# Moving the next layer's keys and values behind the expert slots, and the ternary weights into an earlier region, in a four-layer gated cross-attention kernel

## The chip, the cores and the metric

The kernel runs on one core of a Trainium2 chip. The metric is the device time of one execution in microseconds (us). Before the change it is 1820.37 us, the median of three runs (1815.41 to 1821.47).

## What is computed

The input `x` holds 8 sequences of 256 positions with 256 features; a context of the same shape supplies keys and values. Four layers follow one another. Each adds a gated cross-attention (16 heads of 16 features) and then a gated feed-forward part:

```python
x = x + jnp.tanh(g_xattn[0]) * _L0_xattn_ref(_layernorm(x, axis=-1), ctx_1024, ctx_1024, mask_Bx1xSxS2_ik1)
x = x + jnp.tanh(g_ffn[0]) * _L0_ffn_ref(_layernorm(x, axis=-1), ...)
x = x + jnp.tanh(g_xattn[1]) * _L1_xattn_ref(_layernorm(x, axis=-1), ctx_1024, ctx_1024, ...)
x = x + jnp.tanh(g_ffn[1]) * _L1_ffn_ref(_layernorm(x, axis=-1), L1_ffn_Wr, L1_ffn_W1, L1_ffn_b1, L1_ffn_W2, L1_ffn_b2)
x = x + jnp.tanh(g_xattn[2]) * _L2_xattn_ref(_layernorm(x, axis=-1), ctx_1024, ...)
x = x + jnp.tanh(g_ffn[2]) * _L2_ffn_ref(_layernorm(x, axis=-1), ...)
x = x + jnp.tanh(g_xattn[3]) * _L3_xattn_ref(_layernorm(x, axis=-1), ctx_1024, ...)
x = x + jnp.tanh(g_ffn[3]) * _L3_ffn_ref(_layernorm(x, axis=-1), L3_ffn_w1, L3_ffn_conv_w, L3_ffn_conv_b, L3_ffn_w2)
```

The feed-forward parts of layers 1 and 2 choose two of eight experts for each of the 2048 tokens. That of layer 1 has 1024 hidden units an expert:

```python
logits = x_flat @ Wr
w, ind = jax.lax.top_k(logits, K)
w = jax.nn.softmax(w, axis=-1)
combine = jnp.einsum('tke,tk->te', jax.nn.one_hot(ind, E, dtype=x.dtype), w)

def body(acc, params):
    W1e, b1e, W2e, b2e, ce = params
    h = jax.nn.gelu(x_flat @ W1e + b1e, approximate=False)
    y = h @ W2e + b2e
    return (acc + ce[:, None] * y, None)
```

That of layer 2 does the same with 512 hidden units and a norm of its own. That of layer 3 rounds its weights to -1, 0 and 1, scaled by the mean of their magnitudes, so all of a weight matrix has to be summed before it is used.

## The kernel before

**Stages.** Region 1 holds attention layers 0 and 1, feed-forward 0 and the routing of layer 1 (0 to some 620 us). The first expert layer follows (to 922 us), then region 2, attention layer 2 with the routing of layer 2 (to 1226), the second expert layer (to 1390), and region 3, attention layer 3 with the ternary feed-forward (to the end). Below, "seam 1" and "seam 2" are the two passages from an attention layer to an expert layer.

**Attention.** `attention` (L223) works through one batch element after another ("job"), 16 heads each. The clock of its plan is the unit: one unit is one head of one element. `plan(at, f)` (L600) puts a piece of work at a unit number into `todo`, and `run` issues, for each unit, the scores (`sc`), the probabilities (`st`, exponentials `pT`), the values (`po`) and then that unit's pieces. The order of PE's matmuls is pinned: `mm` and `turn` keep them in program order. The order on DVE, ACT and SP isn't pinned; a scheduler places those instructions, apart from single ones wrapped in `pin`. Indirect gathers on POOL are pinned.

**Setting up a layer.** `setup(l)` (L234) fetches the four weight matrices and the biases, and also forms the bias product: `pgb`, up to three pairs of matmuls of the broadcast value bias with `wo`, plus the output bias, scaled by DVE into `gb`. For the layer after an expert layer it can't be planned inside that layer's own region; it goes into the list `early`. So do the keys and values of that layer's first two elements, K by `proj("k", 0)` and `proj("k", 1)`, V by `vals(0)` and `vals(1)`. `early` thus has nine entries: the setup, four for element 0 and four for element 1. `tail(early, end)` (L1387) gives each of them a unit past the end of the region (offsets 11, 12 to 15, and 23 to 26).

**The K stack.** After both halves of K, `stack` (L259) splits them into three bf16 pieces (`pc_k`, lines L201 to L204, on POOL unless another engine is named), writes them to DRAM (`dr_k`, 384 KB, L281) and reads them back rearranged with six DMAs (`kstack`, L288). All of these are issued on SP. Q goes the same way (`pc_q`, `dr_q`, `qstack`); for the first element after an expert layer in two halves, on DVE.

**Routing.** `routing` (L771) treats four blocks of 512 tokens, two elements each. Its steps stand at units counted from the block's end: `norm`, `normT` (transposes `pt_f`), `out` (router logits `plf`), `choose` (a chain of small DVE steps on the logits, ending in `rtf_run`), `weigh`, `rank` (matmuls `rankf`), and `place` and `tabulate` for both halves (matmuls `tabf` into `rt_table`). The last block's steps lie past the region's end, among `early`.

**Slots and experts.** `slots` (L958) sums the tokens of each expert (matmul `tot`), derives the expert of each slot of 128 tokens (`sl_...`, `wrow`) and the token at each place (matmul `tok`, cast to `toki`), and where each token's results will be (`rt_si`). `experts` then gathers expert weights (`we`) and tokens (`xg`) by indirect DMAs on POOL, transposes the tokens (`ptg`, `xgT`), and runs `phg`, the activation `hg` and `yg`; results (`ysb`) are stored to DRAM (`yd`, by SP). At the start of the next region each element gathers its two results a token (`yg<-yd`) and adds them to `x` (L1158).

**Ternary weights.** `ffn3` (L1170) has `ternary`, which returns for each of two matrices `fetch` (1 MB by SP, `f3raw`, L1191 to L1193), `total` (the sum of magnitudes on DVE, `wab`, L1200), `mean`, and four `quarter` steps that round. They are handed to the second expert layer as `between`, each with the number of the tile at which it is issued.

Of the kernel before, what the change touches and what calls it, by code (L numbers as in the profile page):

```python
# [17 lines left out]
B, S, D = 8, 256, 256  # L18
NH, DK = 16, 16
# [12 lines left out]
AHEAD, VLAG = 3, 1  # L32
# [6 lines left out]
def kernel(ctx: ExitStack, tc: tile.TileContext, a: dict, out: bass.AP):  # L39
# [20 lines left out]
    nc = tc.nc  # L60
# [18 lines left out]
    for b in range(B):  # L79
        for i in range(2):  # L80
            t = 2 * b + i
# [52 lines left out]
    tg = const.tile([P, 8], F32, tag="tg", name="tg")  # L134
    nc.scalar.activation(tg, graw, AF.Tanh)

    def load(name, shape, src):
        t = const.tile(shape, F32, tag=name, name=name)
        nc.scalar.dma_start(t, src)
        return t  # L140

    def row(name):
        t = small.tile([1, D], F32, tag="row", name=f"row_{name}", bufs=1)
        nc.scalar.dma_start(t, a[name].rearrange("(o n) -> o n", o=1))
        return t
# [77 lines left out]
    def attention(layers):  # L223
# [7 lines left out]
        pool = None  # L231
        lay = {}

        def setup(l):  # L234
            y = lay[l] = {"bq": None, "bk": None}
            for n in "qkvo":
                w = awpool.tile([P, DC, D], F32, tag=f"w{n}", name=f"w{n}{l}")
                nc.sync.dma_start(w, a[f"L{l}_w{n}"].rearrange("(c p) o -> p c o", p=P))
                y[n] = w
            bv = None  # L240
            if l in (1, 3):
                y["bq"] = load(f"bq{l}", [P, DC], a[f"L{l}_bq"])
                nc.vector.tensor_scalar(y["bq"], y["bq"], 1.0 / DK**0.5, None, ALU.mult)
                y["bk"] = load(f"bk{l}", [P, DC], a[f"L{l}_bk"])
                bv = load(f"bv{l}", [P, DC], a[f"L{l}_bv"])


            bo = row(f"L{l}_bo")
            pb = bank(ps_m, "m", f"pgb{l}")[:, :D]
            if bv is not None:  # L250
                for c in range(DC):
                    bvb = keep.tile([P, P], F32, tag="bvb", name=f"bvb{l}_{c}", bufs=2)
                    nc.vector.tensor_copy(bvb, bv[:, c : c + 1].to_broadcast([P, P]))
                    mm(pb, bvb, y["o"][:, c, :], c == 0, False)
            mm(pb, ones[0:1, :], bo, bv is None, True)
            y["gb"] = keep.tile([P, D], F32, tag="gb", name=f"gb{l}")
            nc.vector.tensor_scalar(y["gb"], pb, tg[:, l : l + 1], None, ALU.mult)
# [36 lines left out]
        lead = layers[0] > 0  # L294

        def prep(j, l, b):
# [96 lines left out]
            def proj(s, oc):  # L393

                if oc == 0:
                    o["p"] = bank(ps_m, "m", f"p{s}_{n}").rearrange("p (c s) -> p c s", c=DC)
                    o["t"] = keep.tile([P, DC, S], F32, tag=f"{s}T", name=f"{s}T_{n}")
                src = o["xs"] if s == "q" else ctxT[b]
                for c in range(DC):
                    mm(  # L400
                        o["p"][:, oc, :], lay[l][s][:, c, oc * P : (oc + 1) * P], src[:, c, :],
                        c == 0, c == DC - 1,
                    )
                bias = lay[l][f"b{s}"]
                scale = 1.0 / DK**0.5 if s == "q" else 1.0
                dst = o["t"][:, oc, :]
                if bias is not None:
                    nc.scalar.activation(  # L408
                        dst, o["p"][:, oc, :], AF.Identity, bias=bias[:, oc : oc + 1], scale=scale
                    )  # L410
                elif s == "q":
                    nc.scalar.mul(dst, o["p"][:, oc, :], scale)
                else:
                    nc.scalar.copy(dst, o["p"][:, oc, :])
                if s == "q" and lead and j == 0:

                    o["qs"] = stack(o["t"], s, j, oc, nc.vector)
                elif oc:
                    o[f"{s}s"] = stack(
                        o["t"], s, j, engine=nc.vector if s == "q" and lead and j == 1 else None  # L420
                    )

            def vals(i):
# [168 lines left out]
        todo, early = {}, []  # L592
# [7 lines left out]
        def plan(at, f, *args):  # L600
            todo.setdefault(at, []).append(lambda: f(*args))

        for j, (l, b) in enumerate(jobs):
            if l and b == 0:
                if j:
                    plan(NH * (j - 2) - AHEAD - 6, setup, l)
                else:
                    early.append(lambda l=l: setup(l))
            for at, f in prep(j, l, b):
                plan(NH * (j - 2) - AHEAD + at, f)  # L610
            for c in range(DC):
                at = slot[NH * j + HC * c + HC - 1] + 1
                plan(at, parts, j, c)
                plan(at + (3 - (c == 0) if j == 0 else 4), rows, j, c)
            for at, f in finish(j, l, b):
                plan(NH * (j + 1) + at, f)
# [154 lines left out]
    def routing(l, pool, xd, gate, at0):  # L771
# [22 lines left out]
        def block(blk):  # L794
# [140 lines left out]
            def tabulate(h):  # L935
# [12 lines left out]
            at = at0 + NH * (2 * blk + 2)  # L948
            return [
                (at + 11, norm), (at + 19, lambda: normT(0)), (at + 20, lambda: normT(1)),  # L950
                (at + 22, out), (at + 23, choose), (at + 26, weigh), (at + 30, rank),
                (at + 32, lambda: place(0)), (at + 36, lambda: tabulate(0)),
                (at + 37, lambda: place(1)), (at + 41, lambda: tabulate(1)),
            ]

        return w, [(at0, load_weights)] + [q for blk in range(NB) for q in block(blk)]
# [213 lines left out]
    def ffn3(home):  # L1170

        nh = 8
        w = {}

        def hbuf(name):
            return home.tile([P, nh, S], F32, tag="f3h", name=name, bufs=2)
# [5 lines left out]
        def ternary(n, at):  # L1182
# [35 lines left out]
            def quarter(k):  # L1218
# [4 lines left out]
                    q[:, k * BLK : (k + 1) * BLK], t, RND, None, ALU.subtract  # L1223
                )

            return [(0, fetch), (at, total), (at + 1, mean)] + [
                (at + 2 + k, lambda k=k: quarter(k)) for k in range(4)
            ]

# [143 lines left out]
        def pieces(pool):  # L1373
            return [q for b in range(B) for q in element(pool, b)]

        return [(0, load_weights)] + ternary(1, 8) + ternary(2, 16), pieces

    def moe(l, nh, nsets, apart, w, xd, between=(), scale=None):
        with tc.tile_pool(name=f"c{l}", bufs=1) as pool:
            with tc.tile_pool(name=f"rt{l}", bufs=1) as tmp:  # L1380
                rows = slots(l, pool, tmp, w, nsets)
            with tc.tile_pool(name=f"f{l}", bufs=1) as tiles:
                return experts(l, tiles, xd, w["c"], rows, nh, scale, between, nsets, apart)

# [1 line left out]

    def tail(early, end):  # L1387

        at = [11, 12, 13, 14, 15, 23, 24, 25, 26]
        return [(end + k, f) for k, f in zip(at, early)]  # L1390

    early, run = attention((0, 1))
# [1 line left out]
    with tc.tile_pool(name="r1", bufs=2) as pool:  # L1394
        w, pieces = routing(1, pool, xd[0], tg[:, 5:6], NH * B)
        run(pool, ffn0(pool) + pieces + tail(early, 2 * NH * B))
    ahead = moe(1, 8, 3, True, w, xd[0])
    early, run3 = attention((3,))
    with tc.tile_pool(name="r2", bufs=2) as pool:
        w, pieces = routing(2, pool, xd[1], tg[:, 6:7], 0)  # L1400
        run2(pool, pieces + tail(early, NH * B), ahead)
    with tc.tile_pool(name="f3w", bufs=1) as home:
        weights, pieces = ffn3(home)
        ahead = moe(2, 4, 5, False, w, xd[1], weights, w["nw"])
        with tc.tile_pool(name="r3", bufs=2) as pool:
            run3(pool, pieces(pool), ahead)


def _layout(inputs):
# [85 lines left out]
```

## Time and profile before

| what | us |
|---|---|
| median of three runs | 1820.37 |
| the profiled execution | 1816.64 |
| its span, first to last instruction | 1814.8 |
| first expert layer, PE without a break | 647.2 to 920 |
| last yd store of the first expert layer | 922.60 |
| first nm of attention layer 2 | 949.75 |
| wo for the bias product, issue at seam 2 | 1191.18 |
| second expert layer, PE without a break | 1244.6 to 1390 |

The profiled execution is one of the kernel's runs; times of single instructions come from it. TensorE's mean granted clock over it was 0.898. The busy rows cut the span into 40 slices of 45 us, one digit each, in tenths:

```profile
DVE  4655554444767511111137767752422767778777
ACT  0354544555556133333314544512231256555641
POOL 2352232232330244343334453014553445554452
DMA  6654222222541444242224535027341444222000
GB/s 165 150 152 99 69 60 59 60 60 59 129 131 30 112 150 138 88 135 85 85 71 111 132 96 140 17 78 244 99 149 56 129 100 102 66 56 57 7 6 18
```

The slices from 14 to 20 are the first expert layer: DVE has little to do there. Slice 28 (1225 to 1270 us) holds the start of the second expert layer and the greatest DMA traffic of the kernel, 244 GB/s. A row of the timeline reads: start, length, engine, line, operation, output and inputs, shapes, count; in brackets how long the engine stood idle before it, and what ended that.

### The profile page before, as it was taken

What the parts mean: (1) busy time and instruction counts of PE and PEld (TensorE: products, weight loads), DVE (VectorE), ACT (ScalarE), POOL (GpSimd) and SP (SyncE); (2) the same over time, 40 slices, a digit from 0 to 9 for tenths busy, and PEclk for the clock granted to TensorE, in tenths of its full rate; (3) what the DMA queues carried; (4) which work ended last, traced back from release to release, by engine and by line L of the source; (5) the groups of instructions that cost most, each with busy time, mean ns of one, the idle gap of its engine ahead of it and who ended that gap; (6) DMA issues with size and microseconds to landing.
All of it is one profiled execution on the core that took longest, in us unless ns stands there. A gap on an engine that the chain in (4) does not pass through costs nothing.

```text
span 1814.8 us, 27468 instructions
## 1 busy us (share of the span) xinstructions
PE 1446.9 (80%) x9888; PEld 1097.3 (60%) x9918; DVE 946.7 (52%) x2918; ACT 742.2 (41%) x1629; POOL 679.9 (37%) x816
## 2 busy tenths in 40 slices
PE   1689888999998599999957888866997587776653
PEld 1356666676665399999944555546996454454432
DVE  4655554444767511111137767752422767778777
ACT  0354544555556133333314544512231256555641
POOL 2352232232330244343334453014553445554452
PEclk9899999999999799999978988977998788888876
DMA  6654222222541444242224535027341444222000
GB/s 165 150 152 99 69 60 59 60 60 59 129 131 30 112 150 138 88 135 85 85 71 111 132 96 140 17 78 244 99 149 56 129 100 102 66 56 57 7 6 18
DMA packets 101116, 170.11 MB, mean 94 GB/s; under 512 B 26642, under 2 KB 85141, under 8 KB 90197
## 3 DMA queue, kind: packets, MB, share of 16 engines
q1 hardware_dynamic: 71759, 113.93, 25.7%
q0 software_dynamic: 23664, 52.81, 8.9%
q10 hardware_dynamic: 5558, 1.63, 0.4%
q8 instruction: 78, 1.28, 0.3%
q14 instruction: 57, 0.47, 0.1%
HBM read 224.69 MB, written 41.68 MB: 147 GB/s over the span
## 4 chain that ended last, share of the span: by engine, by line
PE 59%; DVE 20%; DMA 8%; POOL 5%; issue 4%; ACT 3%; SPq 1%; ACTq 0%; POOLq 0%; DVEq 0%
PE phg L192 11%; PE yg L192 11%; PE po L192 5%; PE y_f L192 4%; PE st L192 4%; PE ph_f L192 4%; PE sc L192 4%; PE pv L192 3%; PE pk L192 3%; DVE nm L479 3%; PE pq L192 3%; DMA qstack<-mt 2%; DVE ms L474 2%; DMA kstack<-dr_k_None 1%; DMA xg<-xd,toki 1%
## 5 line engine op out<-in xcount | busy, mean ns | idle before, releaser
L523 ACT ACTIVATE pT<-st 128x512 f32<-128x512 f32 x512 | 298.9, 597 | 286.7 <-PE st L192 244.8
L479 DVE TENSOR_REDUCE nm<-sc 128x2 f32<-128x512 f32 x384 | 256.9, 681 | 119.7 <-PE sc L192 118.7
L192 PE MATMUL sc<-kstack,qstack 112*128 112x256 bf16 x1024 | 213.1, 297 | 95.5 <-DMA kstack<-dr_k_None 28.1
L1105 ACT ACTIVATE hg<-phg,we 128x128 f32<-128x128 f32 x468 | 133.5, 368 | 283.9 <-issue 259.6
L192 PE MATMUL st<-qstack,kstack 115*128 115x256 bf16 x1024 | 210.2, 290 | 44.3 <-ACT pT L523 23.6
L192 PEld LDWEIGHTS phg<-xgT,we 128*128 128x128 f32 x1872 | 224.3, 195 | 7.2 <-DVE xgT L1087 1.8
L192 PE MATMUL phg<-xgT,we 128*128 128x128 f32 x1872 | 225.8, 278 | 2.1 <-DVE xgT L1085 1.0
L192 PE MATMUL yg<-we,hg 128*128 128x256 f32 x936 | 214.6, 380 | 0.0
L192 PEld LDWEIGHTS <-qstack 112*128 112x128 bf16 x1024 | 101.7, 106 | 160.1 <-issue 120.9
L192 PEld LDWEIGHTS yg<-we,hg 128*128 128x128 f32 x936 | 172.2, 191 | 20.0
L192 PE MATMUL po<-pT,va 128*32 128x256 f32 x2048 | 155.0, 422 | 0.9
L192 PEld LDWEIGHTS <-kstack 115*128 115x128 bf16 x1024 | 105.0, 103 | 71.1 <-issue 37.3
L474 DVE CUSTOM_DVE_ANT_0 ms<-sc,mb 128x256 f32<-128x256 f32 x256 | 107.2, 419 | 70.2 <-PE sc L192 60.2
L1118 DVE TENSOR_TENSOR ysb<-yg,we 128x256 f32<-128x256 f32 x78 | 33.0, 424 | 169.3 <-PE yg L192 163.6
L169 POOL TENSOR_TENSOR rsr_ff<-rsv_ff,nhalf 128x4 f32<-128x4 f32 (+2 forms) x24 | 24.4, 1017 | 237.5 <-DVE rsv_ff L167 129.4
L192 PEld LDWEIGHTS po<-pT,va 128*32 128x32 f32 x2048 | 57.6, 117 | 64.3 <-issue 42.1
L1085 DVE COPY xgT<-ptg 128x256 f32<-128x256 f32 x39 | 16.5, 424 | 140.0 <-PE ptg L197 140.0
L1036 POOL DMA_INDIRECT xg<-xd,toki x78 | 74.7, 958 | 24.0 <-issue 23.2
L1036 POOL DMA_INDIRECT yg<-yd,rt_si x64 | 63.0, 984 | 51.4 <-issue 29.9
L1036 POOL DMA_INDIRECT we<-in_L_ffn_wa,wrow x39 | 38.8, 996 | 85.5 <-ACT hg L1105 73.0
L192 PE MATMUL ph_f<-xT_f,f0w 128*128 128x256 f32 x288 | 67.1, 390 | 2.8 <-DVE nm L479 2.0
L192 PE MATMUL pv<-wv,ctxT 128*128 128x256 f32 x192 | 59.7, 439 | 12.0 <-ACT kT L408 7.4
(254 smaller groups left out, 2516.3 us busy)
## 6 DMA issues: line engine op xcount, KB each, us to landing
kstack<-dr_k_None SPq DMA_DIRECT2D x160, 128.0 KB
qstack<-dr_q_None SPq DMA_DIRECT2D x60, 256.0 KB
dr_k_None<-pc_k SPq DMA_DIRECT2D x32, 384.0 KB
dr_q_None<-pc_q SPq DMA_DIRECT2D x30, 384.0 KB
qstack<-dr_q_None SPq DMA_DIRECT2D x30, 384.0 KB
yd<-ysb SPq DMA_DIRECT2D x78, 128.0 KB
kstack<-dr_k_None SPq DMA_DIRECT2D x32, 256.0 KB
xd<-fxn_f SPq DMA_DIRECT2D x8, 512.0 KB
```

Of the source, the lines that this page charges most:

```text
L169: pw = nc.gpsimd.tensor_tensor(rs, ve, nhalf[:, :k, :n], ALU.pow)
L192: pin(nc.tensor.matmul(out, lhsT=lhsT, rhs=rhs, start=start, stop=stop, skip_group_check=True))
L474: nc.vector.tensor_tensor_reduce(masked, sc[:, i, :], o["bias"][:, i, :], -1.0, 3.0e38, ALU.add, ALU.min, o["nm"][:, i, h : h + 1],)
L479: nm = nc.vector.tensor_reduce(o["nm"][:, :, h], sc, AX.X, ALU.max, negate=True)
L523: pin(nc.scalar.activation(pT[u], st, AF.Exp))
L1036: return nc.gpsimd.indirect_dma_start(out=dst, out_offset=None, in_=src, in_offset=bass.IndirectOffsetOnAxis(ap=rows, axis=0), **kw,)
L1085: nc.vector.tensor_copy(xT, pv)
L1105: nc.scalar.activation(h[:, hc, :], ph[:, k, :], AF.Gelu, bias=w[:, n1 - nh + hc : n1 - nh + hc + 1],)
L1118: nc.vector.tensor_tensor(ys, py, w[:, nh * D :], ALU.add)
```

## The change

Five things are changed.

- `setup` is cut in two. `setup` fetches; the new `bias` forms the bias product. `early` has ten entries.
- In `tail`, six units are given: 11 for the setup, 24 for the bias product, 23 and 24 for the two halves of element 0's K, and 34 and 38 for those of its V. The other four entries, K and V of element 1, are handed to `moe`, which issues them after `slots`.
- The K stack of element 1 (and not only the Q stack) is split on DVE where the layer follows an expert layer.
- The routing steps from `weigh` on come 2 to 7 units sooner, in every block.
- The two fetches of ternary weights are taken out of the second expert layer and planned at unit 96 of region 2; for this, their pool is opened ahead of region 2's. The weights' own small loads move from tile 0 to tile 4 of the second expert layer.

```diff
-            bo = row(f"L{l}_bo")
+            y["bo"], y["bv"] = row(f"L{l}_bo"), bv
+
+        def bias(l):
+
+
+            y = lay[l]
+            bo, bv = y["bo"], y["bv"]
             pb = bank(ps_m, "m", f"pgb{l}")[:, :D]
             if bv is not None:
                 for c in range(DC):
...
-                        o["t"], s, j, engine=nc.vector if s == "q" and lead and j == 1 else None
+                        o["t"], s, j, engine=nc.vector if lead and j == 1 else None
...
                     plan(NH * (j - 2) - AHEAD - 6, setup, l)
+                    plan(NH * (j - 2) - AHEAD - 6, bias, l)
                 else:
-                    early.append(lambda l=l: setup(l))
+                    early += [lambda l=l: setup(l), lambda l=l: bias(l)]
...
-                (at + 22, out), (at + 23, choose), (at + 26, weigh), (at + 30, rank),
-                (at + 32, lambda: place(0)), (at + 36, lambda: tabulate(0)),
-                (at + 37, lambda: place(1)), (at + 41, lambda: tabulate(1)),
+                (at + 22, out), (at + 23, choose), (at + 24, weigh), (at + 27, rank),
+                (at + 28, lambda: place(0)), (at + 31, lambda: tabulate(0)),
+                (at + 31, lambda: place(1)), (at + 34, lambda: tabulate(1)),
...
-        w = {}
+        w, fetches = {}, []
...
-            return [(0, fetch), (at, total), (at + 1, mean)] + [
+            fetches.append(fetch)
+            return [(at, total), (at + 1, mean)] + [
...
-        return [(0, load_weights)] + ternary(1, 8) + ternary(2, 16), pieces
+        return fetches, [(4, load_weights)] + ternary(1, 8) + ternary(2, 16), pieces
...
-    def moe(l, nh, nsets, apart, w, xd, between=(), scale=None):
+    def moe(l, nh, nsets, apart, w, xd, early, between=(), scale=None):
         with tc.tile_pool(name=f"c{l}", bufs=1) as pool:
             with tc.tile_pool(name=f"rt{l}", bufs=1) as tmp:
                 rows = slots(l, pool, tmp, w, nsets)
+                for f in early:
+                    f()
...
-        at = [11, 12, 13, 14, 15, 23, 24, 25, 26]
+        at = [11, 24, 23, 24, 34, 38]
         return [(end + k, f) for k, f in zip(at, early)]
...
-    ahead = moe(1, 8, 3, True, w, xd[0])
-    early, run3 = attention((3,))
-    with tc.tile_pool(name="r2", bufs=2) as pool:
-        w, pieces = routing(2, pool, xd[1], tg[:, 6:7], 0)
-        run2(pool, pieces + tail(early, NH * B), ahead)
+    ahead = moe(1, 8, 3, True, w, xd[0], early[6:])
+    early3, run3 = attention((3,))
     with tc.tile_pool(name="f3w", bufs=1) as home:
-        weights, pieces = ffn3(home)
-        ahead = moe(2, 4, 5, False, w, xd[1], weights, w["nw"])
+        fetches, weights, pieces3 = ffn3(home)
+        with tc.tile_pool(name="r2", bufs=2) as pool:
+            w, pieces = routing(2, pool, xd[1], tg[:, 6:7], 0)
+            pieces += [(NH * (B - 2), f) for f in fetches]
+            run2(pool, pieces + tail(early3, NH * B), ahead)
+        ahead = moe(2, 4, 5, False, w, xd[1], early3[6:], weights, w["nw"])
         with tc.tile_pool(name="r3", bufs=2) as pool:
-            run3(pool, pieces(pool), ahead)
+            run3(pool, pieces3(pool), ahead)
```

## The prediction

> **What bounds the kernel now.** I read the page first, then busy time by stretch, then the timeline of both seams where an attention layer gives way to an expert layer, and last the chain of waits behind the first seam's end.
>
> ```profile
> span 1814.8 us, 27468 instructions
> PE 1446.9 (80%) x9888; PEld 1097.3 (60%) x9918; DVE 946.7 (52%) x2918; ACT 742.2 (41%) x1629; POOL 679.9 (37%) x816
> PEclk9899999999999799999978988977998788888876
> ...
> PE 59%; DVE 20%; DMA 8%; POOL 5%; issue 4%; ACT 3%; SPq 1%; ACTq 0%; POOLq 0%; DVEq 0%
> ```
>
> PE is the bound: 80% busy, 59% of the chain. PE's work is the same after the change, so only its idle time and its clock can move. The stretches show where these are:
>
> ```profile
> 600.00:650.00 50.00, 31.45 (x158) 24.71 (x158) 17.45 (x86) 10.09 (x28) 21.23 (x22) 0.73 0.67 216
> 650.00:920.00 270.00, 270.00 (x1859) 254.66 (x1858) 31.39 (x74) 84.46 (x296) 101.88 (x104) 1.00 0.29 94
> 920.00:985.00 65.00, 31.64 (x160) 21.54 (x160) 38.55 (x93) 12.81 (x25) 30.43 (x35) 0.71 0.38 104
> ...
> 1190.00:1245.00 55.00, 28.46 (x105) 19.71 (x106) 21.08 (x100) 6.05 (x13) 18.55 (x19) 0.63 0.62 182
> 1245.00:1390.00 145.00, 143.79 (x997) 135.31 (x995) 44.92 (x107) 44.54 (x156) 67.08 (x68) 1.00 0.38 122
> ```
>
> (Window, length, busy PE, PEld, DVE, ACT, POOL, then clock, DMA share, GB/s.) Inside the expert layers PE never stops. The idle time is in three holes: seam 1 (600-650, 18.6 us idle at clock 0.73), the start of attention layer 2 (920-985, 33.4 us), and seam 2 (1190-1245, 26.5 us at 0.63). The change works on all three. Seam 2 in the timeline:
>
> ```profile
> 1206.26 1.95 PE L192 MATMUL plf<-wr,xT_f 128*128 128x8 f32 x16
> ...
> 1214.63 0.30 PE L192 MATMUL rankf<-rtf_both,before 128*128 128x32 f32 x2
> ...
> 1220.52 0.54 PE L192 MATMUL tot<-rtf_run,ones 128*128 128x8 f32 x2
> ...
> 1224.23 0.42 SPq L1193 DMA_DIRECT2D f3raw<-in_L_ffn_w  x1
> ...
> 1228.04 0.97 POOL L1036 DMA_INDIRECT xg<-xd,toki  x1 [0.31 <-issue]
> ...
> 1238.67 0.66 PE L197 MATMUL ptg<-ident,xg 128*128 128x128 f32 x2 [13.89 <-DMA xg<-xd,toki]
> ...
> 1239.84 3.78 PE L192 MATMUL phg<-xgT,we 128*128 128x128 f32 x16 [0.52 <-DVE xgT L1087]
> ```
>
> Two things are to be seen. Between the router's logits (plf, ends 1208.2) and its ranks (1214.63) PE runs K and V of element 1, while DVE, done with the choice at 1211.9, waits 3.25 us for rankf. And the first token gather, issued at 1228.04, feeds PE only at 1238.67, 10.5 us later. At seam 1 the same gather takes 630.27 to 635.16. The difference is what stands in the DMA engines: from 1226 to 1232 queue 1 holds 101% of the engines' time at only 134 GB/s, with the K stack's reads and f3raw; the gathers' queue moves nothing.
>
> ```profile
> 929.03 3.46 DMA yg<-yd,rt_si
> 932.58 0.50 DVE x L1158
> ...
> 944.91 4.08 DMA qstack<-dr_q
> 949.13 1.96 PE sc L192 x8
> ```
>
> This chain says that at the start of layer 2 each gather, vector step and stack read of the first element counts at full length.
>
> [...] the first phg took 3.78 us, a later one 1.95. [...] at seam 2 the gathers saw no packet for some 5 us behind queue 1. [...] the gathers moved 414 GB/s in 632-648[...].
>
> **The change part by part** (negative = faster; sums against the profiled run's 1816.64 us, span 1814.8, which is 3.7 below the median of 1820.37).
>
> *Element 1's K and V behind the slots; bias product later.* At both seams PE's order was: last output, bias product, K0, V0, eight transposes, plf, K1, V1, rankf, tables, tot, tok. It becomes: last output, eight transposes, plf, K0 with the bias product in it, rankf, tables, V0, tot, tok, K1, V1. So plf no longer waits for K0 and V0, and rankf no longer for K1 and V1. At seam 1 the normed rows set the transposes (DVE done with them at 604.67, some 1.2 sooner now, as the third block's last tables no longer stand in the attention's tail: 0.39 of PE, 0.28 of DVE and their waits); 2.1 of transposes and logits later plf ends, at about 605.6, gain 3.2. The choice takes DVE 3.7 (608.89 to 612.6), so rankf can be at 609.4 instead of 616.50: 7.1. But V0's two pairs now stand in front of tot, at half clock 4.4 us (1.9 + 1.9 and the evictions of 0.37 between). Net start of gathers 2.6 us earlier (4.4 if the clock stays full). At seam 2 fxn is done at 1198.94 less 1.2, plf at 1200; K0 and the bias product follow, 2.08 + 2.05 + 1.22 + 2.08 = 7.4 at half clock, so rankf comes at about 1207.6 instead of 1214.63: 7.0, less 4.4 is 2.6. The scaling of the bias product stands in DVE's order inside the choice, which so waits for PE to 1205.4; six short steps of 0.2 remain, done at 1206.7, within K0's second half: 0, up to +1 at seam 1.
>
> *What the gathers then meet.* Seam 1: K1's store (384 KB, 1.1 us of all engines) and its six reads (896 KB in 8 KB packets of 0.5 us: 110 x 0.5 / 16 = 3.4) used to be over before the gathers began; now they fall among them, where the engines are full. PE runs without a break from ptg 2 on:
>
> ```profile
> 630.27 0.97 POOL L1036 DMA_INDIRECT xg<-xd,toki  x1 [0.30 <-issue]
> ...
> 636.34 5.69 PE L192 MATMUL phg<-xgT,we 128*128 128x128 f32 x32 [0.52 <-DVE xgT L1085]
> ...
> 646.94 0.41 PE L197 MATMUL ptg<-ident,xg 128*128 128x128 f32 x2 [0.34 <-DMA xg<-xd,toki]
> ```
>
> Its xg lands 2.6 earlier and up to 4.5 later: +1.9 if all of it stands ahead, -2.6 if none. [...] I take 0, between -3 and +2.
>
> Seam 2: f3raw is no longer there and K1's reads come some 3 us after the first gather rather than before it. With seam 1's 6.3 us from first weight gather (628.69) to landing, xg 0 is there at 1226.64 - 2.6 + 6.3 = 1230.3 instead of 1238.5, 8.2 earlier[...]. K1's 4.5 us of DMA then delay the next experts' weights: a set is 1.18 MB, 2.8 us at 414 GB/s, against 3.73 us of PE for a tile, so the fifth tile's weights come about 1246 and PE would want them at 1245. Some 1 us is given back: -7 (-10 to -4).
>
> *K split of element 1 on DVE instead of POOL.* Four vector operations of about 0.45 to 0.67, 2.2 us, after rt_si; POOL's four took 3.5 and stood ahead of gathers. Nobody waits for DVE there: 0.
>
> *Ternary weights.* Planned for unit 96 of region 2, but with nothing to wait for the two 1 MB fetches stand in SP's order right behind the first onesb row (924.50), ahead of dr_q; they are issued at about 925.5, with the yg gathers (925.25 to 929.97). Packets as they ran at seam 2 (4 KB ones 100 in a us, 1 KB ones 340) make 2.6 + 3.0 = 5.6 us. Taking turns, yg's last landing is 0.5 late; standing behind as at seam 2, 4. I take 1.5. The two sums of magnitudes (wab, 2.27 us each, 1244.43 before) move with the data onto DVE between the splits of the first q: one delays the second half's cast by 2.27 - 0.99 (DVE's idle time there) = 1.28, the other its last piece by 2.27. DVE's next, x and xn of element 1, move by 3.5 and the first nm from 949.75 to about 951.9: +2.2. Together +3.7 (+1 to +7). In the second expert layer they are gone from DVE; the one wait within it, 0.93 for xg at 1269.94, comes 8 us after the second of them (1262.1) held up a row of ysb, whose release the gathers follow: -0.9 (to 0).
>
> *Routing times.* weigh to tabulate come 2 to 7 units sooner in all four blocks. In the last ones that is counted above. In the other blocks only 5 score units, not 8, lie between plf and rankf, while the choice took 9.2 us there (542.8 to 552.0), with PE already waiting 0.48 for it. Three units are 3 x 1.09; three nm less inside the choice give back 3 x 0.68: 1.2 of new wait each, half of which comes off the later wait of sc for nm (1.73 at 556.5): 2 x 0.6 = +1.2 (-1 to +5).
>
> Sum: 0 - 7 + 3.7 - 0.9 + 1.2 = -3.0. The same off the median, 1820.4 - 3.0: 1817 us.
>
> **The rivals.** A, the forecast: both seams gain but layer 2's start gives part back: 1817, with its own range 1811 to 1822.
>
> B, the cover holds everywhere: seam 1 keeps its 2.6, seam 2 8.2 to 10, the fetch costs nothing as yg used only part of the engines, and wab falls where DVE would wait for the stacks anyway (nothing but nm follows). -2.6 - 9 - 0.9 + 0 = -12.5: 1808. For it: PE was idle 33 us in 920-985 and DVE 26. Against it: the chain goes through x, xn and nm there, so those steps aren't covered.
>
> C, slower: the queue in front of the first element. If the 2 MB stand ahead of yg as f3raw stood ahead of xg at seam 2, all four gathers are held, x comes 5 us late, wab another 2 to 3 on top, and the q and K stores behind in the same queue follow: +8. With K1's reads delaying seam 1's third tile by 2 and seam 2 giving back 5, +8 + 2 - 4 = +6: 1826. It decides from the point where yg's last landing comes over 4 us late. For it: the 5 us without a packet at 1228-1233. Against it: there 8 KB stack packets were ahead as well, and yg's first gather is issued at the same moment as the fetch.
>
> D: the routing times cost in all blocks more than the seams bring. It would have to be over 5 us, thrice what I find; its chance is in C's.
>
> **How the numbers follow.** A 0.42, B 0.34, C 0.24. The time is A's, 1817. For 8 in 10 the range goes to B's time and somewhat short of C's far end: 1805 to 1827. A measurement of this kernel tells 0.3% (5.5 us) from no change: nearly all of B and a fifth of A are faster than 1815 (0.42), most of A and a little of B and C same (0.37), the rest of C slower (0.21).
>
> **What would show it.** Right: from plf's end to rankf some 4 us at seam 1 and 7.5 at seam 2, with K0 alone between; V0 just before tot; the first ptg of the second expert layer some 8 us nearer to the last matmul of attention layer 2, phg there at 2 us; the first nm of layer 2 some 31 us after the last yd store, not 27.2 (949.75 - 922.60); two wab of 2.27 us before it. Wrong: yg landing over 4 us late (C), or unchanged distances at the start of layer 2 (B); an xg 2 at seam 1 that ends PE's last wait more than 3 us sooner or later than 0.34 said; rank waits over 2 us in the blocks within the regions.

## The result, and the profile after

The changed kernel took 1830.55 us in the median of 8 runs (1822.86 to 1838.76), the kernel before 1816.87 in the median of 8 (1812.77 to 1821.47): a ratio of 1.0066, with a 95% interval of 1.0039 to 1.0093. It is about 12 us slower, where 3 us faster were predicted, and it lies above the predicted range. Its profiled execution took 1831.92 us.

The page of the kernel after, the same four lines as were shown of before:

```profile
span 1830.1 us, 27467 instructions
PE 1461.7 (80%) x9888; PEld 1105.6 (60%) x9918; DVE 957.2 (52%) x2926; ACT 742.5 (41%) x1629; POOL 674.2 (37%) x808
...
PEclk9999999999999699999968989968999689788876
...
PE 54%; DVE 20%; issue 8%; DMA 8%; POOL 7%; ACT 2%; SPq 1%; POOLq 0%; ACTq 0%; DVEq 0%
```

PE runs the same 9888 matmuls and is busy 14.8 us longer, at a mean granted clock of 0.894 instead of 0.898 (0.62 instead of 0.73 at seam 1). In the chain PE has lost 5 points, and issue and POOL have gained 6. These shares don't tell the loss, though: the fastest kernel below (g1_best) has PE 54%, issue 7% and POOL 7%. Three of the stretches (window, length, busy PE, PEld, DVE, ACT, POOL, clock, DMA share, GB/s):

```profile
600.00:650.00 50.00, 35.11 (x142) 25.97 (x142) 19.82 (x84) 9.16 (x26) 15.89 (x16) 0.62 0.52 179
...
920.00:985.00 65.00, 31.69 (x140) 22.72 (x138) 36.94 (x79) 10.63 (x23) 27.85 (x32) 0.68 0.39 112
...
1245.00:1390.00 145.00, 137.86 (x928) 127.97 (x927) 41.14 (x103) 42.13 (x143) 72.78 (x75) 0.97 0.48 153
```

At seam 1 PE is busy 3.7 us more with 16 fewer matmuls, as the clock fell from 0.73 to 0.62. The second expert layer, which kept PE at 143.8 of 145 us, now shows 137.9; of the idle time 1.2 us are the end of seam 2, whose first phg comes at 1249.28 (0.69 of wait for its xg and 0.52 for xgT), the rest is the layer's own.

Where the 15.3 us between the two profiled spans arose, by the ends of the same instructions in both traces (after minus before). The last column is a second profiled execution of the changed kernel, after_again, against the same trace of before:

| stage, and the instructions that bound it | us | again |
|---|---|---|
| start to the last output of region 1 (py) | -3.0 | +1.0 |
| seam 1, to the first ptg | +4.4 | +4.3 |
| first expert layer, to its last ysb | +2.8 | +2.5 |
| start of layer 2, to its 48th head (pT) | +10.2 | +9.1 |
| rest of region 2, to the last py | -0.8 | -9.7 |
| seam 2, to the first phg | -4.2 | -3.8 |
| second expert layer, to its last ysb | +6.0 | +5.8 |
| region 3 | -0.1 | +3.2 |

In region 1, 5 us were gained in the first 120 us, which the change doesn't touch, and 1.8 in the second execution: executions differ by that much there. So single stages are read to a few us only, and what decides is the timed ratio. The seams and the expert layers agree in both executions: seam 1 with its layer loses 7.2 and 6.7, seam 2 with its layer 1.9 and 2.0. The start of layer 2 loses 9 to 10 in both, but in the second one the rest of region 2 gives all of it back, so a lasting loss in region 2 isn't shown.

Of the stages that agree, only seam 2 gained. At seam 1, the timeline (start, duration, engine, line, operation, and in brackets the wait before it), first of the kernel before:

```profile
606.90 1.95 PE L192 MATMUL plf<-wr,xT_f 128*128 128x8 f32 x16
...
616.64 0.39 PE L192 MATMUL rankf<-rtf_run,ones 128*128 128x32 f32 x2
...
616.84 0.38 SPq L281 DMA_DIRECT2D dr_k_None<-pc_k  x1
...
619.39 2.63 SPq L288 DMA_DIRECT2D kstack<-dr_k_None  x6
...
622.38 0.54 PE L192 MATMUL tot<-rtf_run,ones 128*128 128x8 f32 x2
```

Then of the kernel after:

```profile
601.40 3.57 PE L192 MATMUL plf<-wr,xT_f 128*128 128x8 f32 x16
...
608.07 0.48 DVE L261 TENSOR_SCALAR gb<-pgb,tg 128x256 f32<-128x256 f32 x1 [1.52 <-PE pgb L192]
...
611.19 1.15 POOL L202 TENSOR_TENSOR res_k<-kT,pc_k 128x512 f32<-128x512 f32 x1
611.27 1.10 DVE L878 TENSOR_TENSOR rtf_run<-rtf_run,rtf_both 128x8 f32<-128x8 f32 x1
...
613.20 0.64 PE L192 MATMUL rankf<-rtf_run,ones 128*128 128x32 f32 x2 [1.28 <-DVE rtf_run L878]
...
619.54 2.02 PE L192 MATMUL pv<-wv,ctxT 128*128 128x256 f32 x4
...
622.01 2.07 PE L192 MATMUL pv<-wv,ctxT 128*128 128x256 f32 x4 [0.46 <-ACT va L435]
623.88 0.43 PE L192 MATMUL tot<-rtf_run,ones 128*128 128x8 f32 x2
```

Two things are seen here. The logits are not at 1.95 us but at 3.57: with K0 and V0 moved behind them, PE was busy 2.0 of the 5 us ahead of them, where it had been busy 4.2, and its granted clock is 0.50 there and was 1.00 before. And the choice, which took DVE 3.7 us from the last logit to rtf_run, takes 9.3: DVE waits 1.52 for the bias product; a step of weigh waits 1.04 for ACT, whose rtf_e stands behind the eviction of K0's second half (610.07); and of rtf_run's four steps, 0.16 each elsewhere, one takes 1.10 and two together 1.31 while POOL splits K0. So the ranks end 16.9 us after the last py, where they ended 17.1 after it before: nothing was gained, and V0's 4.3 us in front of tot are a plain loss. At seam 2 the ranks end 4.6 sooner after the last py, but V0 takes 4.2 of that, and the DVE steps from the ranks' end to the first table take 4.1 instead of 2.0, as POOL now splits K0 beside them: tot ends 1.5 later.

The second loss is in SP's order and in the DMA engines. SP's issues in the second expert layer of the kernel after, then the DMA's queues in 1251 to 1259 (packets, MB, share):

```profile
1247.64 0.38 SPq L285 DMA_DIRECT2D dr_k_None<-pc_k  x1
1260.81 2.71 SPq L292 DMA_DIRECT2D kstack<-dr_k_None  x6
1263.89 6.87 SPq L1124 DMA_DIRECT2D yd<-ysb  x3
```

```profile
q0 software_dynamic: 380, 2.64, 88.7%
q1 hardware_dynamic: 372, 0.37, 13.1%
```

K1's store is issued at 1247.64; the six reads that wait for it start 13.2 us later, where K1's pair at seam 1 of the kernel before, ahead of the gathers, is 2.6 apart (616.84 to 619.39). The queues moved about the same number of packets, but the store's hold 1 KB and the gathers' 7 KB in the mean: about one row of the store went for each gather packet. In the single us from 1251 on they are 37 and 39, 41 and 42, 57 and 57. Behind the reads, in SP's order, stand the yd stores, which need nothing of K1: the first is issued at 1263.89, its ysb was done at 1259.15. PE's waits in the rest of that layer, for the kernel after:

```profile
PE ptg L197 <- DMA xg<-xd,toki: 4.0, 3, 1.9
PE yg L192 <- DVE ysb L1123: 0.9, 1, 0.9
```

Before, the one wait of the layer was 0.9 us for xg.

### The profile page after: what moved, and what is told of

Same layout as the page of the kernel before. It is cut to its first block, busy times and chain, and to the rows that moved or that the text cites. A ratio compares the mean times of both kernels' runs of the same rounds, so it can differ in the third digit from the quotient of the medians.

```text
span 1830.1 us, 27467 instructions
## 1 busy us (share of the span) xinstructions
PE 1461.7 (80%) x9888; PEld 1105.6 (60%) x9918; DVE 957.2 (52%) x2926; ACT 742.5 (41%) x1629; POOL 674.2 (37%) x808
## 4 chain that ended last, share of the span: by engine, by line
PE 54%; DVE 20%; issue 8%; DMA 8%; POOL 7%; ACT 2%; SPq 1%; POOLq 0%; ACTq 0%; DVEq 0%
PE yg L192 11%; PE phg L192 11%; PE y_f L192 4%; PE po L192 4%; PE ph_f L192 4%; PE st L192 3%; DVE nm L483 3%; PE sc L192 3%; PE pk L192 3%; PE pv L192 2%; PE pq L192 2%; DVE ms L478 2%; DMA xg<-xd,toki 2%; DMA kstack<-dr_k_None 2%; DVE h_f L1307 1%
## 5 line engine op out<-in xcount | busy, mean ns | idle before, releaser
L1041 POOL DMA_INDIRECT xg<-xd,toki x78 | 74.7, 958 | 24.0 <-issue 22.9
L192 PE MATMUL pq<-xs,wq 128*128 128x256 f32 x192 | 66.8, 481 | 4.3 <-ACT qT L412 1.7
```

What stands on the lines that cost most here:

```text
L192: pin(nc.tensor.matmul(out, lhsT=lhsT, rhs=rhs, start=start, stop=stop, skip_group_check=True))
L1041: return nc.gpsimd.indirect_dma_start(out=dst, out_offset=None, in_=src, in_offset=bass.IndirectOffsetOnAxis(ap=rows, axis=0), **kw,)
```

## The experiments

Each kernel was timed in five rounds beside the kernel before; ratios are to it, with 95% intervals, so that values from different groups of runs compare through it. Each expectation names the theories that it weighs. Each trace is one execution, and as the order on DVE, ACT and SP isn't pinned, an edit can also move instructions that it doesn't name.

**The parts alone.** The first three take the kernel before and make one part of the change; the fourth takes the change and leaves the fetch where it was.

Only the fetch is moved (the diff's lines on `fetches`):

```diff
-            return [(0, fetch), (at, total), (at + 1, mean)] + [
+            fetches.append(fetch)
+            return [(at, total), (at + 1, mean)] + [
...
+            pieces += [(NH * (B - 2), f) for f in fetches]
```

> The kernel before with one part alone: the ternary fetches moved into region 2 (with their pool and the load at tile 4). If the fetch is the main loss (theory 1, read from the trace of after: yg late by 2.5, first nm by 4.2, the third element's K stack colliding with the yg gathers for another 5), layer 2 starts about 10 us later and seam 2 gains 3 to 5 without f3raw: 4 to 7 us slower than before. If the seams are the main loss (theory 2), within 2 us of before or faster.

Only the routing times are made earlier:

```diff
-                (at + 22, out), (at + 23, choose), (at + 26, weigh), (at + 30, rank),
+                (at + 22, out), (at + 23, choose), (at + 24, weigh), (at + 27, rank),
...
```

> The kernel before with the earlier routing times alone. Theory 1 of the times: each block inside a region makes PE wait 1 to 2 us for the choice, in sum 2 to 4 us slower than before. Rival: the attention's end free of the third block's tables is worth as much, within 1 us of before.

Only the seams: bias product apart, element 1's K and V behind the slots, its K split on DVE:

```diff
-        at = [11, 12, 13, 14, 15, 23, 24, 25, 26]
+        at = [11, 24, 23, 24, 34, 38]
...
-                        o["t"], s, j, engine=nc.vector if s == "q" and lead and j == 1 else None
+                        o["t"], s, j, engine=nc.vector if lead and j == 1 else None
```

> The kernel before with the seam's part alone: K0 and the bias product behind the router's logits, K1 and V1 behind the slots with the split on DVE; routing times and ternary fetches as before, so that V0's two pairs stand between ranks and tables. If the seam part is a loss by itself (cold clock for the logits, the choice waiting for the bias product, the K1 stack among the gathers), 4 to 8 us slower than before. If only its combination with the earlier routing times loses (V0 as a block in front of tot), within 2 us of before.

The change without the fetch:

```diff
-            fetches.append(fetch)
-            return [(at, total), (at + 1, mean)] + [
+            return [(0, fetch), (at, total), (at + 1, mean)] + [
```

> The changed kernel with the ternary fetches put back where they were. Theory 1: layer 2's start is as in before (27 us from the last yd store to the first nm, no wait of 8 us for a K stack), 4 to 7 us faster than the changed kernel, 7 us or so slower than before. Theory 2 (seams and expert layers lose what is lost): within 2 us of the changed kernel, 12 slower than before.

| kernel | seams | times | fetch | ratio | interval |
|---|---|---|---|---|---|
| e1_fetch | - | - | moved | 0.9989 | 0.9973 to 1.0006 |
| e3_times | - | early | - | 1.0005 | 0.9986 to 1.0023 |
| e4_seam | moved | - | - | 1.0060 | 1.0037 to 1.0084 |
| e2_nofetch | moved | early | - | 1.0125 | 1.0093 to 1.0157 |
| after | moved | early | moved | 1.0066 | 1.0039 to 1.0093 |

The seams are what costs: 11 us, more than the 4 to 8 expected. The times cost nothing alone, but 6.5 thousandths on top of the seams (12 us). The fetch, which rival C blames, is no loss: alone it can't be told from nothing, and in the change it takes off some 6 thousandths, so that e2_nofetch is 11 us slower than the change, which neither theory had. The trace of e1_fetch has both halves that were forecast: the layer's start loses 4.5 us (the last ysb 4.3 ahead of before, the first nm of layer 2 0.2 behind), and seam 2 gains 6.1. The trace of e2_nofetch shows why it is worth more beside K1's late stack. PE's longest wait in its second expert layer:

```profile
PE phg L192 <- DVE xgT L1092: 10.1, 2, 9.6
```

DVE stands in wab (10.18 us of wait for f3raw), and xgT behind it: that fetch is issued at 1241.28, 0.7 us after K1's store in the same queue, and wab can start at 1261.78 only.

**V0 in front of tot.** Two kernels, each with one edit to the changed one: V0's pairs go behind the slots too, or the old routing times come back, by which the two pairs fall between ranks and tables.

```diff
-        at = [11, 24, 23, 24, 34, 38]
+        at = [11, 24, 23, 24]
...
-    ahead = moe(1, 8, 3, True, w, xd[0], early[6:])
+    ahead = moe(1, 8, 3, True, w, xd[0], early[4:])
```

> The changed kernel with V0's two pairs behind the slots as well. If V0 in front of tot costs its 4 us a seam and PE is idle anyway while the first gathers are under way: tot 4 us sooner at both seams, 4 to 8 us faster than the changed kernel. Rival: what comes sooner meets K1's stack among the gathers all the same: under 3 faster.

```diff
-                (at + 22, out), (at + 23, choose), (at + 24, weigh), (at + 27, rank),
+                (at + 22, out), (at + 23, choose), (at + 26, weigh), (at + 30, rank),
...
```

> The changed kernel with the old routing times, which puts V0's two pairs between the ranks' and tables' matmuls, where PE waits for DVE, instead of as a block in front of tot. If that block is what the times and the seam cost together: tot 4 us sooner at both seams, no loss in the expert layers, 8 to 11 us faster than the changed kernel, within 3 of before. If the early times are worth something by themselves, slower than the run with V0 behind the slots by 2 to 4.

With V0 behind: 1.0005 (0.9992 to 1.0019), no longer to be told from before. With the old times: 1.0024 (1.0010 to 1.0038). The change itself was run again with the second of them:

> The changed kernel once more, beside the two others on one chip: 10 to 14 us slower than before, with the same losses by stage (seam 1 up to the first ptg 4, first expert layer 3, layer 2's start 9 to 10, second expert layer 6, a gain of 4 at seam 2).

It gave 1.0079 (1.0054 to 1.0105). So f3_v0_behind takes off 6 to 7 thousandths and h1_old_times 4 to 5.5. From the last py to tot's end, seam 1 took 22.9 us before, 27.4 after, 23.1 in f3_v0_behind and 23.8 in h1_old_times; seam 2 took 29.9, 31.4, 27.4 and 26.5. At tot both kernels are so 8 us nearer over the two seams, of the 8 to 13 that the ratios give back. At the first ptg of layer 1 and the first phg of layer 2 it is 8.2 in h1_old_times and 5.8 in f3_v0_behind. e4_seam and e2_nofetch, too, differ by the times alone, and there by 8.3. The early times put tot behind V0, and that is most of their cost on top of the seams.

f3_v0_behind gains more elsewhere. The order on SP differs: in both kernels, the first yd store of the second expert layer is issued ahead of K1's reads. In f3_v0_behind that layer then loses nothing (1.2 ahead of before at its first phg, 2.2 at its end), 7.0 less than in the change; in h1_old_times it still loses 6.0, 4.0 of them in one wait for xg.

**K1's stack among the gathers.** If the reads in front of the yd stores are what costs, swapping these two in SP's order gives the layer's loss back, with V0 and all else of the program as in the change. The store stays where it is; only the six reads are issued behind the first yd store:

```diff
+            def reads(hold):
+                ...
+            if keep_:
+                late.append(lambda: reads(pin))
...
+                between = list(between) + [(1, f) for f in late]
```

> The changed kernel with one swap in SP's queue: the six reads of element 1's K stack stand behind the first result store (yd) of the expert layer instead of ahead of it; the split and the store of the stack stay where they are. If the loss in the second expert layer (6 us from the first phg to its end) is that first yd store waiting behind reads which wait for the small-packet store, its end is 4 to 6 us sooner, the first layer's 0 to 2. If the loss is the stack's packets among the gathers, wherever SP has them, nothing changes, within 2 us of the changed kernel.

SP's order in the second expert layer is now:

```profile
1243.63 0.38 SPq L285 DMA_DIRECT2D dr_k_None<-pc_k  x1
1254.43 0.34 SPq L1135 DMA_DIRECT2D yd<-ysb  x1
1256.06 2.63 SPq L295 DMA_DIRECT2D kstack<-dr_k_None  x6
```

The layer's loss against before fell to 0.6 us (5.5 late at its first phg, 6.1 at its end), where the change, run beside it, lost 5.8 (3.2 to 9.0). The timed ratio is 1.0056 (1.0037 to 1.0075) against 1.0079: in the right direction, but the intervals overlap, so the swap's worth in total is not known better than from nothing to some 7 us. Nor is SP's order the whole cause, for h1_old_times has the same order and loses 6.0:

```profile
1237.06 0.38 SPq L285 DMA_DIRECT2D dr_k_None<-pc_k  x1
1248.28 0.34 SPq L1124 DMA_DIRECT2D yd<-ysb  x1
1249.90 3.05 SPq L292 DMA_DIRECT2D kstack<-dr_k_None  x6
```

```profile
1257.28 0.66 PE L197 MATMUL ptg<-ident,xg 128*128 128x128 f32 x2 [4.03 <-DMA xg<-xd,toki]
```

From 1252 to 1257 queue 1, which carries the reads, took 66 to 97% of the engines in each us, while the tokens that PE waited for were under way. So the store, the reads and what stands behind them in SP's order can each cost there; how the 6 us divide between them isn't shown.

Moving the stack altogether was tried in four steps. First element 1's store and reads to tile 10 of the expert layer (its kT buffer is held until then), then both stacks there with V0 behind the slots, then this with the old times and the fetch held in its place, last both stacks at tiles 32 and 34 in the change as it is:

```diff
+                elif oc and s == "k" and lead and j == 1:
+                    o["ks"] = stacks[s][j % 3]
+                    late.append(lambda t=o["t"]: stack(t, s, j, engine=nc.vector, keep_=True))
...
+                between = list(between) + [(10 + 2 * i, f) for i, f in enumerate(late)]
```

> The changed kernel with the store and the reads of element 1's K stack held back to the tenth tile of the expert layers (its split on DVE and the matmuls stay). If the store among the gathers is what the expert layers lose (its small packets wait in turn with the gathers' 9 KB ones, SP's reads and yd stores wait behind it): ptg of the third tile and the expert layers' ends are 2 to 3 us sooner at the first and 5 to 6 at the second, 7 to 9 us faster than the changed kernel. Rival: the matmuls of K1 and V1 behind the slots, or the later gathers themselves, are the loss; then within 2 us of the changed kernel.

> The changed kernel with both elements' K stacks held back (tiles 10 and 12, split on DVE) and V0's two pairs behind the slots too. If V0 in front of tot costs 4 us a seam, and POOL's split of K0 stretches DVE's steps of the choice and the ranks by about 1 us each, two a seam: tot 5 to 6 us sooner at each seam, in sum 8 to 14 faster than the run before it. Rival: gathers are bound by DMA at seam 1 and by their latency at seam 2, under 4 faster.

> As the run before it, with the old routing times and with the fetches held at unit 96. If the early times cost 2 us or so in the regions' own blocks and the fetch at the region's start 4: 4 to 8 faster again, under 1808. If the seam's new order needs the early times, no faster.

> The changed kernel with nothing changed but both K stacks' split, store and reads at tiles 32 and 34. If K stack traffic is the whole loss of the expert layers (2.8 and 6 us) and POOL's split 1 to 2 a seam: 9 to 12 us faster than the changed kernel, within 3 of before; left over are V0 in front of tot, the cold logits and layer 2's start. Rival: no more than the 3 to 6 that the run with K1 alone held back brought.

f2_stack_late gave 1.0051 (1.0033 to 1.0069), f4_stack_late_v0 1.0025 (1.0010 to 1.0040), f5_all 1.0013 (1.0000 to 1.0026), g2_stacks_end 1.0027 (1.0013 to 1.0042). f2_stack_late is 3 to 5 us faster than the change by these ratios, not 7 to 9, with intervals that overlap; f4_stack_late_v0 is 5 faster than it, not 8 to 14. But f2_stack_late shows in its stages what K1's stack costs at the layer's head. With its store and reads at tile 10, the second expert layer loses 1.8 us instead of 6.0 and the first 1.2 instead of 2.8, and store and reads are 2.65 apart, as they were ahead of the gathers:

```profile
1286.69 0.43 SPq L285 DMA_DIRECT2D dr_k_None<-pc_k  x1
1289.34 2.63 SPq L292 DMA_DIRECT2D kstack<-dr_k_None  x6
```

With both stacks, at tiles 10 and 12, it is otherwise: the layer loses 8.1 in f4_stack_late_v0 and 10.3 in f5_all, where the second stack's reads come 14 us after its store:

```profile
1280.35 0.43 SPq L285 DMA_DIRECT2D dr_k_None<-pc_k  x1
1283.69 10.59 SPq L1129 DMA_DIRECT2D yd<-ysb  x3
1294.38 2.71 SPq L292 DMA_DIRECT2D kstack<-dr_k_None  x6
```

This isn't a store that takes turns with gathers: from 1288 to 1294 the DMA engines carry next to nothing (their share over 1290 to 1300 is 0.56, no more than the 5.6 us from the reads' issue on would fill). The reads stand behind yd stores, and one of these waits 9.7 us for its ysb, which DVE writes behind the xgT of two later tiles, at 1293.05, though its yg ended at 1286.94. What put DVE's steps in this order was not tested. At tiles 32 and 34 of the change, where the last gathers are under way, g2_stacks_end's layer gains 1.3 (2.5 late at its first phg, 1.2 at its end). In this kernel K0's split is off POOL, too, and tot ends 1.0 us sooner than in the change at seam 1 and 0.3 at seam 2.

**The start of layer 2.** The fetch, held at unit 96, behind the last element's K stack, in the kernel before:

```diff
-                nc.sync.dma_start(
+                pin(nc.sync.dma_start(
```

> The kernel before with the ternary fetches moved and held at unit 96 of region 2, behind the last K stack, so that they no longer stand at the region's start. If the early place at the region's start costs what it seems to (first nm 4.5 us later in the run with the fetch alone) and seam 2's gain of 7 stays: 5 to 10 us faster than before. If the start's loss is hidden later in the region: as the run with the fetch alone, 2 to 4 faster than before.

It gave 0.9979 (0.9963 to 0.9995), some 4 us faster where 5 to 10 were expected, and the two wab fall at 1146.88 and 1157.39. Between the last ysb and layer 2's first nm 0.3 us are lost instead of e1_fetch's 4.5. The intervals of the two kernels overlap, so what holding the fetch is worth in total isn't shown.

**All of it.** f5_all with the stacks at tiles 32 and 34: element 1's K and V and V0 behind the slots, both K stacks at the expert layer's end, the old times, the fetch held.

```diff
-                between = list(between) + [(10 + 2 * i, f) for i, f in enumerate(late)]
+                between = list(between) + [(32 + 2 * i, f) for i, f in enumerate(late)]
```

> The run with everything together (V0 behind the slots, old routing times, fetches held at unit 96) with both K stacks' DMAs at tiles 32 and 34 instead of 10 and 12. If the 9 to 10 us that it lost in the second expert layer came from the second store standing in turn with weight gathers (14 us from its issue to its reads, the yd stores behind it): the layer loses nothing, 8 to 10 faster than that run, 1806 to 1811, faster than the kernel before and than the one with the fetches held. If any place in the layer costs as much: as that run.

1808.38 us, ratio 0.9939 (0.9917 to 0.9960): 11 us faster than the kernel before and, by the ratios, about 23 faster than the change. It is 13 faster than f5_all, from which only the stacks' tiles differ. Its profiled execution is its slowest (1817.69), so its stages tell of places and not of sizes: layer 2's start loses nothing to its 48th head, seam 2 gains 9.4 and the second expert layer 1.9.

## Why the prediction was wrong

*What bounds the kernel: right as to the places.* What is lost for certain lies at the two seams and in the expert layers behind them. The sum had 0 for seam 1 with its layer and -7.9 for seam 2 with its layer; measured were +7.2 and +1.9 (+6.7 and +2.0 in the second execution). These 17 us are as much as the whole distance between -3 forecast and +12 timed. Two steps of the sum failed there.

*First gathers 2.6 us sooner at each seam: wrong, and the step that failed first.* The sum held V0's price right (4.4; measured 4.3 and 4.2) and set against it ranks 7 us sooner, some 1 of it ahead of the last py. After the last py they came 0.2 sooner at seam 1 and 4.6 at seam 2. Its terms were mis-sized. From the last normed row to the logits' end it had 2.1 us, and it took 4.1 at both seams: without K0 and V0 ahead of them the logits alone took 3.57 and 3.42, at a granted clock of 0.50, which the sum applied only to K0 and V0. The choice was taken at 3.7 us, as if it stood alone on DVE; it took 9.3 and 6.4, with gb's wait at 1.52 and 2.03 where the sum had 0 to 1, and at seam 1 with K0's eviction on ACT and its split on POOL in the way. At seam 2 the split fell between ranks and tables, 2.1 us that the sum had at nothing. So tot ended 4.4 later at seam 1 and 1.5 later at seam 2, and the first phg of the second expert layer, which was said at 2 us, took 3.68: its granted clock was 0.54, and that it would be full was my estimate.

*Seam 2's gather without f3raw: right.* From the first weight gather to the first ptg 12.0 us became 6.7; 5.3 gained, where 8.2 less 2.6 were expected of this. e1_fetch shows the gain without the seams' other edits, with 6.1.

*K1's stack among the gathers: the second step that failed.* I priced it by bandwidth, 4.5 us of the engines, took 0 for seam 1 and gave back some 1 us at seam 2. Measured: 2.8 us in the first expert layer and 6.0 in the second; with K1's store and reads at tile 10 (f2_stack_late) 1.2 and 1.8 were left. What was missed is that the store's 1 KB rows went about one for one with the gathers' packets (372 and 380 in 8 us), so that its reads are issued 13 us after it instead of 2.6, and that SP's order holds the yd stores behind these reads (the first for 4.7 us after its ysb). One execution of j1_reads_behind, in which the layer's loss is gone, speaks for the second; h1_old_times, with the same order and 6.0 lost, shows that it is not all.

*Layer 2's start: the size of the fetch was right, and more came that was missed.* The chain of waits of the kernel after:

```profile
933.22 6.00 DMA yg<-yd,rt_si
939.31 0.49 DVE x L1163
...
947.97 2.20 DVE wab L1205
```

The last yg lands after 6.00 us instead of 3.46, the two wab, 2.27 each, stand between the splits, and the first nm comes 31.3 us after the last yd store instead of 27.2: +4.15, where 3.7 was said. Then 6 us more follow that no step named, at the third element's K stack:

```profile
1004.76 0.59 PE L192 MATMUL sc<-kstack,qstack 112*128 112x256 bf16 x2 [8.77 <-DMA kstack<-dr_k_None]
```

Its reads are issued at 994.61 and the next yg gathers at 995.74 to 998.32. The wait is there in after_again (7.6) and in e4_seam (7.7), which has no early fetch, and at most 3.1 in f3_v0_behind, h1_old_times, j1_reads_behind and g1_best; e2_nofetch, with the seams and the times but no early fetch, has none. What decides it was not settled: these kernels differ in when reads and gathers meet, and no run moved that alone. As after_again made up for it within region 2, it need not be part of the timed loss.

*Routing times +1.2: not contradicted.* After the first 120 us, region 1 lost 2 and the rest of region 2 gained 0.8; PE waits 3.1 us for the ranks' inputs in region 1's blocks and 3.6 in region 2's, where it waited 0.5 in each. e3_times, at 0.9986 to 1.0023, is too wide to tell 1.2 us from nothing. Their real cost, tot behind V0, was in the sum under the seams.

*The rivals.* C named the right side and one right mechanism, K1's reads in seam 1's third tile, but decided on the 2 MB in front of yg. That point wasn't reached: yg came 2.5 us late, under the 4 named, and e2_nofetch shows that without the fetch it is slower still. B fails by layer 2's start, where the first nm came 4 us late and not on time, and by both seams. D asked for a cost of the times alone, which e3_times doesn't show. Two figures of these rivals don't fit each other: C's words give 5 us for seam 2 and its sum 4, and D's 5 us are four times the 1.2 found, not thrice; neither changes a choice.

## What to carry to other kernels

When work is moved off the front of a chain, price the chain again as it then stands: the logits, without K0 and V0 ahead of them, ran at a granted clock of 0.50 instead of 1.00, and the choice, which now shares DVE with the bias product and waits for K0's eviction on ACT, took 9.3 us instead of 3.7. K1's store, moved among gathers, was to be priced in packets and not in bytes: 372 of its 1 KB packets took 13.1% of the engines' time, but went beside 380 of 7 KB in 8 us, and the yd store behind its reads in SP's order waited 4.7 us after its ysb. A stack that isn't needed before the next region can go where the gathers end: from tiles 10 and 12 to 32 and 34 it was worth 13 us here.

## What the runs showed of the hardware

Some DVE steps beside an instruction of POOL lasted until that one was over. rtf_run, 0.16 us elsewhere, ran from 611.27 to 612.37 beside POOL's res_k from 611.19 to 612.34; at seam 2 rt_q, with one tensor input, took 1.17 instead of 0.17 beside the same POOL step, and ended at 1225.85, where res_k ended at 1225.83. It was so beside POOL's casts, with one input, too: a step of weigh took 0.56 instead of 0.16 and ended 0.02 after the cast. Other steps beside the same POOL steps kept their length: the 0.69 of nm, a reduction that reads PSUM (507.85 to 508.54), beside res_k (to 508.09), and the 0.28 of two rtf_kk, reductions in SBUF (1224.37 to 1224.65), beside a cast (1223.99 to 1224.60), as at seam 1 without one. What sets the two kinds apart isn't shown. On this path of tiny steps one POOL step cost up to 1 us (rt_q).

In one stretch of the kernel after, 1251 to 1259, two DMA queues moved about a packet for a packet: 380 of one and 372 of the other in 8 us, with 88.7% and 13.1% of the engines' time. At seam 2 of the kernel before it was so in part: the gathers' queue moved none from 1228 to 1233, while queue 1 took 96.7% of the engines, and in the two us from 1234 to 1236 it moved 31 and 46 against the other's 30 and 48.
